# Sign convolutions in blocks of 16 rows across the images, in a fixed order, with shorter steps between the layers

## The chip, the cores and the metric

The kernel runs on one core of a Trainium2 chip, as one launch. The metric is the device time of that core in microseconds (us). The engines are named as in the profile: PE is TensorE's matmul, PEld its weight load, DVE the vector engine, ACT the scalar engine, POOL GpSimd, SP the engine that issues most transfers.

## The reference

The input is `x` of 16 images, 256 channels, 28 x 28 pixels in float32. Four layers follow one another. Cut to what matters here:

```python
# layer 0: sign of x, 3x3 convolution with the signs of the weights, batch norm, residual
y  = sat_conv2d(binary_activation(x), sign(w0)) * mean(abs(w0))   # the scale is per output channel
x  = (y - mean(y)) * rsqrt(var(y) + eps) * gamma + beta + x       # statistics over images and pixels
# layer 1: a 3x3 and a 1x1 convolution with real weights on signs, gates, PReLUs
...
# layer 2: two sign convolutions with batch norms before, between and after
out = sign(batchnorm(x, g1, b1))
out = prelu(binconv(out, w1), a1)          # weights sign(w1) * mean(abs(w1))
out = sign(batchnorm(out, g2, b2))
out = prelu(binconv(out, w2), a2)
x   = prelu(batchnorm(out, g3, b3) + x, a3)
# layer 3: attention over the 784 pixels of each image, then a projection, plus x
```

So there are three sign convolutions of the same size: one in layer 0, two in layer 2. Each is followed by statistics over all images, and nothing of the next part can begin before these are known.

## The kernel before

Channels lie on 128 partitions, in two halves `k` of the input and `mo` of the output. `S` = 28, `N` = 784, `HN` = 392, `HR` = 14, `B` = 16.

A sign convolution adds whole numbers. Of the 18 pairs of input half and tap, 15 are computed with *packed* weights: the signs for one output half plus 4095 times those for the other, so that one matmul serves both. ACT and DVE get the upper number out by rounding, and an *unpack* matmul takes it away again from one half and adds it to the other. The last three pairs are computed plainly, once for each output half.

```python
def sign_conv(pss, pad, w, temp):
    def product(ps, h, lhsT, n, t, start, stop, again=False):
        k, g = CHUNKS[n]
        r, c = divmod(3 * g + t, 3)
        T.matmul(ps[:, h, :HN]..., lhsT=lhsT,                      # line 198
                 rhs=pad[:, k, r + h * HR:r + h * HR + HR, c:c + S], start=start, stop=stop, ...)
    bs = [None, None]
    for h in range(2):                                             # two halves of an image
        for n in range(5):
            for t in range(3):
                product(pss[0], h, w[0][:, n, t, :], n, t, n + t == 0, n + t == 6)
        r, bs[h] = temp("t1"), temp("up", FR)
        A.activation(r, pss[0][:, h, :HN], AF.Identity, bias=rounding, scale=1.0 / PACK)   # line 210
        V.tensor_scalar(bs[h], r, -ROUND, None, ALU.add)           # line 211
    for h in range(2):
        for mo in range(2):
            for t in range(3):
                product(pss[mo], h, w[1][:, t, mo * P:(mo + 1) * P], 5, t, ...)
    for h in range(2):
        for mo in range(2):
            T.matmul(pss[mo][:, h, :HN], lhsT=unpack[mo], rhs=bs[h], start=False, stop=True, ...)  # line 218
```

An image takes 30 packed, 12 plain and 4 unpack matmuls. Each image has a padded buffer of its own (two, in turn), and the order of instructions on each engine is chosen by the framework's scheduler. The weights' signs and their mean absolute values come in six chunks:

```python
def sign(k, g):
    st = sts[k, g] = load_taps(pool, src, k, g, *stage)
    ...                                                            # the sixth chunk: plain signs
    A.activation(sg, st, AF.Sign, saturate=False)                  # line 158
    V.scalar_tensor_tensor(dst[0][:, n], sg[:, :, P:], PACK, sg[:, :, 0:P], ALU.mult, ALU.add)
def add_up(k, g):
    V.tensor_reduce(ab, st.rearrange("p t o -> p o t"), AX.X, ALU.add, apply_absolute_value=True)  # line 169
    part = acc.tile([P, 2], F32, tag="sm", name="sumabs")
    for mo in range(2):
        T.matmul(part[:, mo:mo + 1], lhsT=ab[:, mo * P:(mo + 1) * P], rhs=ones, start=True, stop=True)  # line 172
    ...                                                            # DVE adds part to the total
```

In layer 2 a convolution's result goes through a PReLU, and its statistics are taken:

```python
def conv2(i, b, w, beta):
    pss_ = [conv_ps() for mo in range(2)]
    sign_conv(pss_, pads2[i % 2], w, temp)
    for mo, ps in enumerate(pss_):
        r = ph.tile([P, 2, HN], F32, tag="r", name="r", bufs=3)
        ...
            A.activation(r[:, h], ps[:, h, :HN], AF.Relu, scale=-1.0)                # line 710
            V.scalar_tensor_tensor(p[:, h], r[:, h], beta[:, mo:mo + 1], ps[:, h, :HN], ALU.mult, ALU.add)
            for j in range(h.start, h.stop):
                V.bn_stats(stats[:, mo, 2 * b + j, :], p[:, j, :])                   # line 715
steps = [rest[1]] + both(*sign_weights(ph, w2b, d["w2b"], sf2, pss, ("r", 3)))     # the stage is the buffers of r
sign2a(0)
for i in range(B):
    if i + 1 < B:
        sign2a(i + 1)                                              # also loads image i + 2 from memory
    conv2(i, order[i], w2a, r1)
    if i >= 2 and steps:
        steps.pop(0)()
m, v = mean_var("l2b", stats)
keep_busy(m, 9)
sg2, bg2 = sign_bn("l2b", sf1, m, v, pv("g2"), pv("b2"))
```

`mean_var` aggregates all 32 partial statistics of each half and copies mean and variance; `sign_bn` is a chain of small DVE operations around one square root on ACT. `keep_busy` issues useless matmuls whose operand is made from the mean:

```python
def keep_busy(v, n):
    A.copy(idle[:, 0:2], v)                                        # line 285
    ps = pss.tile([P, 512], F32, tag="sm", name="unused")
    for _ in range(n):
        T.matmul(ps, lhsT=idle[:, 0:P], rhs=idle, start=True, stop=True)   # line 288
```

In the attention each image's denominators are inverted, the values are normalized, and two ACT passes add up the denominators and their inverses so that an overflow is noticed (line 929, tile `junk`).

Of the kernel before, what the change touches and what calls it, by code (L numbers as in the profile page):

```python
# [36 lines left out]
P = 128  # L37
B = 16
# [8 lines left out]

PACK = 4095.0
# [16 lines left out]
def conv_seq_kernel(ctx: ExitStack, tc: tile.TileContext, d: dict, out: bass.AP):  # L65
# [19 lines left out]

    pads = [const.tile([P, 2, S + 2, S + 2], BF16, tag=f"pad{i}", name=f"pad{i}") for i in range(2)]
    for p in pads:
        nc.gpsimd.memset(p, 0.0)

    def float_pads(pool, tag):  # L90
        ps = [pool.tile([P, 2, S + 2, S + 2], FR, tag=f"{tag}{i}", name=f"fpad{i}") for i in range(2)]
        for p in ps:
            nc.gpsimd.memset(p.bitcast(F32), 0.0)
        return ps
# [4 lines left out]
    eye = wpool.tile([P, P], F32, tag="wa", name="eye")  # L99
    make_identity(nc, eye)  # L100
    unpack = [wpool.tile([P, P], FR, name=f"unpack{i}") for i in range(2)]
    for u, f in zip(unpack, (-PACK, 1.0)):
        V.tensor_scalar(u, eye, f, None, ALU.mult)
    rounding = const.tile([P, 1], F32, name="rounding")
    nc.gpsimd.memset(rounding, ROUND)
# [8 lines left out]
    def inv_std(name, var):  # L114

        v, r, t = vtile(name + "_v"), vtile(name + "_r"), vtile(name + "_t")
        V.tensor_scalar(v, var, EPS, None, ALU.add)
        A.activation(t, v, AF.Sqrt)
        V.reciprocal(r, t)
        tt(t, r, r, ALU.mult)  # L120
        tt(t, t, v, ALU.mult)
        V.tensor_scalar(t, t, -0.5, 1.5, ALU.mult, ALU.add)
        return tt(r, r, t, ALU.mult)

    def affine(name, inv, gamma, beta, mean):

        s, c = vtile(name + "_s"), vtile(name + "_c")
        tt(s, gamma, inv, ALU.mult)
        tt(c, mean, s, ALU.mult)
        tt(c, beta, c, ALU.subtract)  # L130
        return s, c
# [13 lines left out]
    def sign_weights(pool, dst, src, total, acc, stage=("st", 2), spare_dve=False):  # L145


        chunks = CHUNKS
        sts = {}

        def sign(k, g):
            st = sts[k, g] = load_taps(pool, src, k, g, *stage)
            n = chunks.index((k, g))
            if n == 5:
                A.activation(dst[1], st, AF.Sign, saturate=False)
                return
            sg = pool.tile([P, 3, 256], BF16, tag="t1", name="sg", bufs=2)
            A.activation(sg, st, AF.Sign, saturate=False)
            V.scalar_tensor_tensor(dst[0][:, n], sg[:, :, P:], PACK, sg[:, :, 0:P], ALU.mult, ALU.add)  # L159

        def add_up(k, g):
            st = sts.pop((k, g))
            ab = pool.tile([P, 256], F32, tag="ab", name="ab", bufs=2)
            if spare_dve:
                A.activation(st, st, AF.Abs)
                nc.gpsimd.tensor_tensor(ab, st[:, 0, :], st[:, 1, :], ALU.add)
                nc.gpsimd.tensor_tensor(ab, ab, st[:, 2, :], ALU.add)
            else:
                V.tensor_reduce(ab, st.rearrange("p t o -> p o t"), AX.X, ALU.add, apply_absolute_value=True)
# [23 lines left out]
    def sign_conv(pss, pad, w, temp):  # L193

        def product(ps, h, lhsT, n, t, start, stop, again=False):
            k, g = CHUNKS[n]
            r, c = divmod(3 * g + t, 3)
            T.matmul(  # L198
                ps[:, h, :HN].rearrange("p (a b) -> p a b", b=S), lhsT=lhsT,
                rhs=pad[:, k, r + h * HR:r + h * HR + HR, c:c + S], start=start, stop=stop,  # L200
                skip_group_check=again,
            )

        bs = [None, None]
        for h in range(2):
            for n in range(5):
                for t in range(3):
                    product(pss[0], h, w[0][:, n, t, :], n, t, n + t == 0, n + t == 6)
            r, bs[h] = temp("t1"), temp("up", FR)
            A.activation(r, pss[0][:, h, :HN], AF.Identity, bias=rounding, scale=1.0 / PACK)  # L210
            V.tensor_scalar(bs[h], r, -ROUND, None, ALU.add)  # L211
        for h in range(2):
            for mo in range(2):
                for t in range(3):
                    product(pss[mo], h, w[1][:, t, mo * P:(mo + 1) * P], 5, t, mo == 1 and t == 0, False, mo == 0)
        for h in range(2):
            for mo in range(2):
                T.matmul(  # L218
                    pss[mo][:, h, :HN], lhsT=unpack[mo], rhs=bs[h], start=False, stop=True,
                    skip_group_check=(mo == 0),  # L220
                )

# [3 lines left out]
    def row_parts(first):  # L226

        return ((0, HR + 1), (HR + 1, S)) if first else ((0, S),)

    def img(ap):  # L230
        return ap.rearrange("p (a b) -> p a b", b=S)

    def mean_var(name, st):

        m, v = vtile(name + "_m"), vtile(name + "_var")
        for k in range(2):
            mv = small.tile([P, 2], F32, tag="mv", name="mv")
            V.bn_aggr(mv, st[:, k].rearrange("p c s -> p (c s)"))
            V.tensor_copy(m[:, k:k + 1], mv[:, 0:1])
            V.tensor_copy(v[:, k:k + 1], mv[:, 1:2])  # L240
        return m, v

    def sign_bn(name, sf, m, v, gamma, beta):

        t = vtile(name + "_sv")
        tt(t, sf, sf, ALU.mult)
        tt(t, t, v, ALU.mult)
        r = inv_std(name, t)
        tt(r, r, sf, ALU.mult)
        return affine(name, r, gamma, beta, m)  # L250
# [7 lines left out]
    stats = const.tile([P, 2, 2 * B, 6], F32, name="stats")  # L258
# [15 lines left out]
    with tc.tile_pool(name="ps_conv", bufs=3, space=PSUM) as psc, \  # L274
# [6 lines left out]
        nc.gpsimd.memset(idle[:, 2:], 0.0)  # L281

        def keep_busy(v, n):

            A.copy(idle[:, 0:2], v)
            ps = pss.tile([P, 512], F32, tag="sm", name="unused")
            for _ in range(n):
                T.matmul(ps, lhsT=idle[:, 0:P], rhs=idle, start=True, stop=True)

        with tc.tile_pool(name="ph1", bufs=1) as ph:  # L290

            pads0 = float_pads(ph, "vs")
# [10 lines left out]
            def sign0(b):  # L303
                for r in row_parts(b == 0):
                    for k in range(2):
                        A.activation(
                            inner(pads0[b % 2], k, *r), img(xs[b][:, k, :])[:, r[0]:r[1]], AF.Sign, saturate=False
                        )

            def quarter(tag, dt=F32):  # L310
                return ph.tile([P, HN], dt, tag=tag, name=tag, bufs=2)
# [3 lines left out]
            sign0(0)  # L315
            for s in signs:
                s()
            load_x(1)

# [24 lines left out]
            steps = [lambda k=k, c=c: w1_step(k, c) for k in range(2) for c in range(3)] + [fw_step] + sums_  # L344
            for b in range(B):
                if b + 1 < B:
                    sign0(b + 1)
                if b + 2 < B:
                    load_x(b + 2)
                n = ph.tile([P, 2, N], I16, tag="n", name=f"n{b}", bufs=2)  # L350
                pss_ = [conv_ps() for mo in range(2)]
                sign_conv(pss_, pads0[b % 2], w0, quarter)
                for mo, ps in enumerate(pss_):
                    for h in range(2):
                        V.bn_stats(stats[:, mo, 2 * b + h, :], ps[:, h, :HN])
                    A.copy(halves(n[:, mo, :]), ps[:, :, :HN])
                nc.gpsimd.dma_start(out=n0d[b], in_=n)
                if b >= 2 and steps:
                    steps.pop(0)()
# [3 lines left out]


            s1, c1 = affine("abn1", inv_std("abn1", pv("a_bn1_3")), pv("a_bn1_0"), pv("a_bn1_1"), pv("a_bn1_2"))
            s2, c2 = affine("abn2", inv_std("abn2", pv("a_bn2_3")), pv("a_bn2_0"), pv("a_bn2_1"), pv("a_bn2_2"))
            s3, c3 = affine("fbn1", inv_std("fbn1", pv("f_bn1_3")), pv("f_bn1_0"), pv("f_bn1_1"), pv("f_bn1_2"))
            s4, c4 = affine("fbn2", inv_std("fbn2", pv("f_bn2_3")), pv("f_bn2_0"), pv("f_bn2_1"), pv("f_bn2_2"))
            cc = tt(vtile("cc"), c2, c4, ALU.add)

            m0, v0 = mean_var("l0", stats)
            keep_busy(m0, 16)
            sc0, bi0 = sign_bn("l0", sf0, m0, v0, pv("g0"), pv("b0"))
            zb1 = tt(vtile("zb1"), bi0, pv("a_move"), ALU.add)

            ra1, ra2, rf2 = (combine("r" + q, pv(q), -1.0, 1.0) for q in ("a_alpha1", "a_alpha2", "f_alpha2"))
            ns1, ns3, nc3, nbi0 = (combine(q, v, -1.0) for q, v in (("ns1", s1), ("ns3", s3), ("nc3", c3), ("nbi0", bi0)))
            zb2 = tt(vtile("zb2"), c2, pv("f_move"), ALU.add)
# [5 lines left out]
            mix_x, mix_y, mix_c, s24 = (const.tile([P, 2, 2], F32, name=n) for n in ("mix_x", "mix_y", "mix_c", "s24"))  # L384
            w_1, w_2, b_1 = (ph.tile(sh, F32, name=n) for sh, n in (([P, 2, P], "se1"), ([P, 256], "se2"), ([64, 1], "seb")))
            hidden = [ph.tile([P, 2], F32, name=f"hidden{i}") for i in range(3)]
            for t in (w_1, w_2, *hidden):
# [819 lines left out]
```

## Time and profile before

The time is 1230.58 us, the median of three runs from 1229.44 to 1232.80. The profiled execution spans 1228.1 us with 15404 instructions.

| Engine | busy us | share | instructions |
|---|---|---|---|
| PE | 1125.3 | 92% | 5940 |
| PEld | 934.6 | 76% | 5944 |
| DVE | 784.3 | 64% | 1405 |
| ACT | 691.5 | 56% | 1047 |
| POOL | 140.9 | 11% | 131 |

The stages, from the timeline (the first useful matmul of a stage to its last): layer 0 from 20.25 to 169.0 us, layer 1 from 179.72 to about 563.5, the two convolutions of layer 2 from 580.96 to 747.3 and from 757.81 to 904.5, the attention from 917.99 to the end. A matmul's record lasts longer than the distance from one start to the next[...]; a short wait of PE doesn't show as idle time, and the distance of the starts has to be read.

### The profile page before, as it was taken

Reading aid. Unit: us, or ns where it says so; the run is one execution under the profiler, and the core shown is the slowest. Engines: PE = TensorE matmul, PEld = TensorE weight load, DVE = VectorE, ACT = ScalarE, POOL = GpSimd, SP = SyncE. Lnnn points to the kernel's source line nnn. Section 1 sums busy time; section 2 is a strip of 40 time slices with the busy share of each in tenths; the row PEclk is TensorE's granted clock in tenths of the full one; section 3 lists DMA queues with packets and bytes.
Section 4 is the critical chain, followed back from the end, with each engine's and each line's share of the span. In section 5 each row is a group of like instructions: output and inputs, shape, how many; then the busy total and the mean of one; then the engine's idle time right before and its main releaser. Section 6 shows DMA issues by size and latency. Waiting matters only on the chain.

```text
span 1228.1 us, 15404 instructions
## 1 busy us (share of the span) xinstructions
PE 1125.3 (92%) x5940; PEld 934.6 (76%) x5944; DVE 784.3 (64%) x1405; ACT 691.5 (56%) x1047; POOL 140.9 (11%) x131
## 2 busy tenths in 40 slices
PE   5999989999999999984987997999979999999995
PEld 4999969999899999983976996999955455455542
DVE  5563359999999998965444544454563665565565
ACT  3564435757676665654534543545547767667642
POOL 2000000000100000001000000000003333324412
PEclk9999999999999999995998998999989999999997
DMA  6454321222221321101322320000003544553512
GB/s 261 147 195 153 123 101 43 77 104 89 109 79 66 119 80 53 46 33 66 131 78 85 125 79 1 1 1 1 1 1 105 132 135 102 158 147 106 143 79 81
DMA packets 25967, 111.61 MB, mean 91 GB/s; under 512 B 3552, under 2 KB 6304, under 8 KB 25888
## 3 DMA queue, kind: packets, MB, share of 16 engines
q1 hardware_dynamic: 20432, 80.85, 18.5%
q0 software_dynamic: 5456, 29.71, 8.6%
q8 instruction: 49, 0.80, 0.3%
q14 instruction: 30, 0.25, 0.1%
HBM read 65.59 MB, written 44.96 MB: 90 GB/s over the span
## 4 chain that ended last, share of the span: by engine, by line
PE 74%; DVE 12%; ACT 10%; issue 2%; DMA 1%; POOL 1%; SPq 0%; ACTq 0%; POOLq 0%; DVEq 0%
PE cv L198 32%; PE cv L468 15%; PE av L898 6%; PE sc L877 5%; PE mi L862 4%; PE sm L935 3%; PE cv L218 2%; DVE x L597 1%; ACT y L543 1%; DVE x L552 1%; ACT junk L929 1%; DVE stats L599 1%; ACT rn L428 1%; PE cv L565 1%; DVE xs L460 1%
## 5 line engine op out<-in xcount | busy, mean ns | idle before, releaser
L468 PE MATMUL cv<-vs,w 128*128 128x392 f32 x1536 | 301.7, 355 | 8.3 <-DVE y L501 7.2
L198 PE MATMUL cv<-fpad,wpk 128*128 128x392 f32 x1440 | 302.3, 358 | 0.8 <-DVE wpk L159 0.8
L468 PEld LDWEIGHTS cv<-vs,w 128*128 128x128 f32 x1536 | 286.2, 190 | 12.7 <-DVE y L501 9.9
L198 PEld LDWEIGHTS cv<-fpad,wpk 128*128 128x128 f32 x1440 | 271.8, 192 | 11.5 <-ACT t L210 7.7
L210 ACT ACTIVATE t<-cv,rounding 128x392 f32<-128x392 f32 x96 | 56.3, 587 | 168.5 <-PE cv L198 165.0
L198 PE MATMUL cv<-fpad,wpl 128*128 128x392 f32 x576 | 138.5, 368 | 13.7 <-DVE p L711 9.7
L198 PEld LDWEIGHTS cv<-fpad,wpl 128*128 128x128 f32 x576 | 105.2, 194 | 32.2 <-ACT t L210 17.4
L211 DVE TENSOR_SCALAR up<-t 128x392 fp32r<-128x392 f32 x96 | 34.8, 362 | 132.6 <-ACT t L210 130.9
L711 DVE SCALAR_TENSOR_TENSOR p<-r,r,cv 128x784 f32<-128x784 f32 (+1 forms) x66 | 63.6, 1002 | 86.2 <-ACT r L710 86.2
L881 ACT ACTIVATE es<-sc 112x784 f32<-112x784 f32 x112 | 86.9, 819 | 47.6 <-PE sc L877 47.5
L877 PE MATMUL sc<-q,k 64*112 64x392 f32 x448 | 90.1, 515 | 6.0 <-ACT es L881 4.4
L898 PE MATMUL av<-es,va 112*64 112x392 f32 x448 | 80.8, 499 | 0.0
L877 PEld LDWEIGHTS sc<-q,k 64*112 64x112 f32 x448 | 36.4, 174 | 47.8 <-ACT es L881 15.7
L869 DVE COPY k<-mi 64x784 f32<-64x784 f32 x16 | 15.6, 976 | 85.0 <-ACT q L868 85.0
L898 PEld LDWEIGHTS av<-es,va 112*64 112x64 f32 x448 | 29.3, 136 | 47.8 <-issue 45.0
L111 DVE TENSOR_TENSOR vs<-pad 128x840 fp32r<-128x840 bf16 (+1 forms) x68 | 64.1, 974 | 0.0
L715 DVE BATCH_NORM_STATS2 stats<-p 128x6 f32<-128x392 f32 x128 | 63.1, 553 | 0.0
L891 POOL TENSOR_TENSOR sum<-sum,es 112x784 f32<-112x784 f32 x32 | 59.7, 1866 | 2.5
L582 ACT ACTIVATE u<-cv,fbn_c,fbn_s 128x784 f32<-128x784 f32 x31 | 31.2, 1005 | 46.3 <-PE cv L565 46.3
L565 PE MATMUL cv<-z,fw 128*128 128x392 f32 x256 | 51.5, 351 | 5.1 <-ACT z L556 5.0
L710 ACT ACTIVATE r<-cv 128x784 f32<-128x784 f32 (+1 forms) x66 | 49.1, 790 | 10.2 <-PE cv L218 7.7
L565 PEld LDWEIGHTS cv<-z,fw 128*128 128x128 f32 x256 | 47.0, 194 | 6.0 <-ACT z L556 5.5
(232 smaller groups left out, 1593.4 us busy)
## 6 DMA issues: line engine op xcount, KB each, us to landing
xs<-in_x_dram SPq DMA_DIRECT2D x32, 784.0 KB, 4.4
x2d<-x POOLq DMA_DIRECT2D x16, 784.0 KB, 3.6
x<-x2d SPq DMA_DIRECT2D x16, 784.0 KB, 4.3
xd<-p SPq DMA_DIRECT2D x16, 784.0 KB, 3.3
out_dram<-p SPq DMA_DIRECT2D x15, 784.0 KB, 4.3
p<-x2d POOLq DMA_DIRECT2D x13, 784.0 KB, 8.6
n0d<-n POOLq DMA_DIRECT2D x16, 392.0 KB, 2.9
n<-n0d SPq DMA_DIRECT2D x16, 392.0 KB, 3.0
```

The source lines that it names most:

```text
L111: V.tensor_tensor(o, a, b, op)
L198: T.matmul(ps[:, h, :HN].rearrange("p (a b) -> p a b", b=S), lhsT=lhsT, rhs=pad[:, k, r + h * HR:r + h * HR + HR, c:c + S], start=start, s ...
L210: A.activation(r, pss[0][:, h, :HN], AF.Identity, bias=rounding, scale=1.0 / PACK)
L468: T.matmul(ps.rearrange("p (a b) -> p a b", b=S), lhsT=w[:, k, c, u, mo * P:(mo + 1) * P], rhs=vs[b % 2][:, u, k, :, c:c + S], start=(n == 0),
L565: T.matmul(ps[:, h, :HN], lhsT=w[:, k, mo * P:(mo + 1) * P], rhs=z2[b][:, k, h * HN:(h + 1) * HN], start=(n == 0), stop=(n == 3),)
L711: V.scalar_tensor_tensor(p[:, h], r[:, h], beta[:, mo:mo + 1], ps[:, h, :HN], ALU.mult, ALU.add)
L715: V.bn_stats(stats[:, mo, 2 * b + j, :], p[:, j, :])
L862: T.matmul(ps[:, h, :HN], lhsT=wqk[:, k, :], rhs=x[b][:, k, h * HN:(h + 1) * HN], start=(k == 0), stop=(k == 1),)
L877: T.matmul(ps[:MC, h, :HN], lhsT=k_[rows, c * MC:(c + 1) * MC], rhs=qs[b][rows], start=True, stop=True)
L881: A.activation(e, ps[:MC, :, :HN], AF.Exp, scale=0.125)
L891: (V if late else nc.gpsimd).tensor_tensor(sums[b, late], sums[b, late], e, ALU.add)
L898: T.matmul(ps[64 * h:64 * h + 64, :HN], lhsT=w, rhs=e[:, h, :], start=start, stop=stop)
```

## The change

The change is in four parts.

- **Blocks.** The padded images are stacked in a ring of three, with one row of zeros between two images. 16 images of 29 rows are 464 rows, or 29 blocks of 16, and a matmul takes one block of 448 columns. A block may lie in two images. Its plain and unpack products come after the next block's packed ones, so that the rounding in between has time.
- **Fixed order.** PE, ACT and DVE issue what a sign convolution emits in the order of the code.
- **Between the layers.** Statistics of the earlier blocks are aggregated ahead (`gather`), the norm has fewer small operations, constants are computed during layer 0, and the useless matmuls need no operand from the statistics.
- **Loads and attention.** The next weights are staged in the buffers of the images, images are loaded at once to where the results will lie, and the attention's passes over the denominators are moved to later places.

The core of the diff, with cuts:

```diff
-    def sign_conv(pss, pad, w, temp):
+    def sign_layer(ring, w, temp, sign, post, steps, moments):
...
+        def packed(j):
+            pss[j] = conv_ps()
             for n in range(5):
                 for t in range(3):
-                    product(pss[0], h, w[0][:, n, t, :], n, t, n + t == 0, n + t == 6)
+                    product(j, 0, w[0][:, n, t, :], n, t, n + t == 0, n + t == 6)
...
+            A.activation(r, pss[j][:, 0, :BN], AF.Identity, bias=rounding, scale=1.0 / PACK)
+            V.tensor_scalar(bs[j], r, -ROUND, None, ALU.add)
+
+        def plain(j):
             for mo in range(2):
                 for t in range(3):
...
+        with tc.manual_schedule(engines={ET.PE, ET.Activation, ET.DVE}):
+            for j in range(NBLK + 1):
+                if j == 0:
+                    sign_image(0)
+                if j < NBLK:
+                    packed(j)
+                if j > 0:
+                    plain(j - 1)
+                    post(j - 1, pss[j - 1], parts(j - 1))
+                if j == NBLK - 2:
+                    moments.gather()
+
+                while done + 1 < B and (j == 0 if done + 1 < RING else ...):
+                    done += 1
+                    sign_image(done)
+                if j >= 2 and steps:
+                    steps.pop(0)()
...
-        def keep_busy(v, n):
-            A.copy(idle[:, 0:2], v)
+        def keep_busy(n):
             ps = pss.tile([P, 512], F32, tag="sm", name="unused")
             for _ in range(n):
-                T.matmul(ps, lhsT=idle[:, 0:P], rhs=idle, start=True, stop=True)
+                tc.keep_in_program_order(T.matmul(ps, lhsT=idle[:, 0:P], rhs=idle, start=True, stop=True))
...
             load_x(0)
-            sign0(0)
-            for s in signs:
-                s()
+            for i in range(3):
+                signs[i]()
             load_x(1)
+            for i in range(3, 6):
+                signs[i]()
+            load_x(2)
...
-            steps = [...] + [fw_step] + sums_
+            steps = [...] + [fw_step] + sums_ + [constants]
...
+            for b in order[3:]:
+                x2[b] = pt[b]
+                nc.sync.dma_start(out=x2[b], in_=x2d[b])
...
+                def post(j, ps, parts):
+                    r = ph.tile([P, 2, BN], F32, tag="r", name="r", bufs=2)
+                    for mo in (slice(0, 1), slice(1, 2)) if j == NBLK - 1 else (slice(0, 2),):
+                        A.activation(r[:, mo], ps[:, mo, :BN], AF.Relu, scale=-1.0)
+                    for at, i, r0, r1, p0 in parts:
+                        n = (r1 - r0) * S
+                        for mo in range(2):
+                            p = pt[order[i]][:, mo, r0 * S:r1 * S]
+                            V.scalar_tensor_tensor(p, r[:, mo, p0:p0 + n], beta[:, mo:mo + 1], ps[:, mo, p0:p0 + n], ...)
+                            V.bn_stats(mom.part(at, mo), p)
...
-            steps = [rest[1]] + both(*sign_weights(ph, w2b, d["w2b"], sf2, pss, ("r", 3)))
+            steps = [rest[1]] + both(*sign_weights(xpool, w2b, d["w2b"], sf2, pss, ("x2", 3), tmp=ph, ab_tag="ab"))
...
-            keep_busy(m, 9)
-            sg2, bg2 = sign_bn("l2b", sf1, m, v, pv("g2"), pv("b2"))
+            keep_busy(30)
+            sg2, bg2 = norm("l2b", mom, pv("g2"), pv("b2"), sf1)
```

The numbers of useless matmuls go from 16, 9, 9 and 16 to 30, 20, 30 and 45. In the attention `watch` (the two ACT passes) is called after the next image's sums, and the last images' denominators come later than before.

## The prediction

> **What bounds the kernel now.** I read the page's chain of work first: TensorE is 74% of it, and line 198, the sign convolutions, is the largest entry. These convolutions are three of the five stages (layer 0 up to 169 us, and two in layer 2), so I asked for the busy time of each engine by stage (columns: window, length, PE, PEld, DVE, ACT, POOL with instruction counts, granted clock, DMA share, GB/s).
>
> ```profile
> PE 74%; DVE 12%; ACT 10%; issue 2%; DMA 1%; POOL 1%; SPq 0%; ACTq 0%; POOLq 0%; DVEq 0%
> ...
> 580.90:747.20 166.30, 152.70 (x765) 142.06 (x764) 77.82 (x142) 76.00 (x103) 0.00 (x0) 0.97 0.27 92
> 757.80:904.50 146.70, 146.58 (x738) 135.97 (x736) 67.99 (x122) 71.22 (x96) 0.00 (x0) 0.99 0.00 1
> 25.00:169.00 144.00, 142.70 (x725) 133.81 (x725) 62.91 (x147) 73.03 (x115) 8.79 (x15) 1.00 0.43 153
> ```
>
> Two of the three stages leave TensorE without idle time; the first convolution of layer 2 takes 166.3 us for the same arithmetic, 19.6 more than the second. So I asked two things of the timeline: what one matmul costs where TensorE never rests, and what happens where it does.
>
> ```profile
> 840.88 2.81 PE L198 MATMUL cv<-fpad,wpk 128*128 128x392 f32 x14
> 843.53 0.92 PE L198 MATMUL cv<-fpad,wpl 128*128 128x392 f32 x4
> 844.37 3.11 PE L198 MATMUL cv<-fpad,wpk 128*128 128x392 f32 x15
> 847.88 0.35 PE L198 MATMUL cv<-fpad,wpk 128*128 128x392 f32 x1
> 848.16 1.40 PE L198 MATMUL cv<-fpad,wpl 128*128 128x392 f32 x6
> 849.40 0.71 PE L218 MATMUL cv<-up,unpack 128*128 128x392 f32 x3
> ```
>
> The first column is the start. 14 starts from 840.88 to 843.53 are 189 ns apart; unpack matmuls, whose moving operand is flat, are 180 apart (849.40 to 849.94 for three). The jump from 847.88 to 848.16 is 0.28: a wait for ACT's rounding, hidden because a record (358 ns) outlasts the distance of two starts. There are two such jumps in an image, and each is followed by another long one; together 0.37 us. An image is 42 x 0.189 + 4 x 0.181 + 0.37 = 9.03 us, against 9.06 in the chain (831.98 to 841.04).
>
> ```profile
> 746.55 0.70 PE L218 MATMUL cv<-up,unpack 128*128 128x392 f32 x3
> 747.11 1.21 ACT L710 ACTIVATE r<-cv 128x784 f32<-128x784 f32 x2 [1.85 <-PE cv L218]
> 747.96 1.56 DVE L711 SCALAR_TENSOR_TENSOR p<-r,r,cv 128x784 f32<-128x784 f32 x2 [2.31 <-ACT r L710]
> 749.44 1.50 DVE L715 BATCH_NORM_STATS2 stats<-p 128x6 f32<-128x392 f32 x3
> ...
> 754.75 3.62 PE L288 MATMUL unused<-idle 128*128 128x512 bf16 x8 [7.50 <-ACT idle L285]
> 756.57 4.40 ACT L689 ACTIVATE fpad<-p,l2b_c,l2b_s 128x420 fp32r<-128x420 f32 x6 [1.80 <-DVE l2b_c L111]
> ```
>
> This is the end of a stage: ReLU, PReLU, statistics, then a chain of 0.16 to 0.20 us operations, and 10.9 us without a useful matmul. The useless ones come after 7.5 us of idleness.
>
> ```profile
> 661.48 2.33 PE L198 MATMUL cv<-fpad,wpl 128*128 128x392 f32 x6 [2.37 <-DVE p L711]
> 664.77 1.04 DVE L169 TENSOR_REDUCE ab<-st 128x256 f32<-128x768 f32 x1 [0.52 <-DMA st<-in_w2b_dram]
> 664.83 0.85 ACT L158 ACTIVATE sg<-st 128x768 bf16<-128x768 f32 x1 [3.75 <-DMA st<-in_w2b_dram]
> 666.65 0.60 PEld L172 LDWEIGHTS sumabs<-ones,ab 128*128 128x128 f32 x4
> 666.83 0.50 PE L172 MATMUL sumabs<-ones,ab 128*128 128x1 f32 x4
> ```
>
> This is the loss of the slow stage: weights of the next convolution are loaded into buffers shared with the ReLU's output, ACT and DVE stand behind the DMA, and TensorE behind both.
>
> [...] useless matmuls of 512 columns start 427 ns apart after 4.3 and 7.5 us of idleness, and the six at 661.48 are slow after only 2.37. [...]
>
> **The change, part by part** (minus is gained, in us).
>
> *Blocks.* A layer goes from 736 matmuls of 392 columns to 29 x 23 = 667 of 448. Of 189 ns, [...] 9 are the rows (189 less 180, for 14 rows); [...] A block is 21 x 0.214 + 2 x 0.204 = 4.90, a layer 142 to 143.5, say 142.7, against 16 x 9.06 = 145.0. The waits for rounding vanish because a block's plain products come one block later. **-2.3 a layer, -7.** In return the second block needs the second image, whose signs ACT takes in fixed order after the first rounding: 0.2 + 0.64 + about 1.4 us. **+2.3 in each layer 2 convolution**, and 0.5 at each stage's end, where the gather (two aggregations of 240 values, some 1.2 each by the 192 values that take 1.0) stands before the last rounding. **+6.**
>
> *Start.* The first image's products before end at 34.1, as if the layer had begun at 34.1 - 9.1 = 25. DVE there does constants and sums before it packs weights (first packing at 19.54, though ACT's first weights land at 6.7). Now those come later. Weights land one per 1.0 us, with an image (2 us) put between: the fifth at about 12.7, then ACT 0.84, packing 0.55; first block done near 15, second at 20. That is a beginning at 20 - 2 x 3.2 = 13.6. **-11.**
>
> *Sums of weights in fixed order.* This is the step that I hold decisive. In an iteration the code emits packed products, plain products of the block before, its post-processing, signs of images, and then a step. A step that sums weights has a reduction on DVE and two small products on TensorE. In fixed order these stand ahead of the next block's products and wait for the reduction, which stands behind the post-processing of products that have only just ended. In layer 2, from the last unpack's start: 0.20 to ACT, ReLU of 896 values 0.91 (0.81 for 784, 0.50 for 392), PReLU and statistics 2 x (0.62 + 0.55) = 2.3 to 2.5, packing 0.55, reduction 1.03, handover 0.1, products 0.47: 5.7, less one distance of 0.2: 5.5 lost. Two of the seven steps pack nothing and lose 4.9: 37.6 in all. In layer 0 there is only statistics ahead (1.1 to 1.3): 0.2 + 1.2 + 1.03 + 0.1 + 0.47 - 0.2 = 2.8, six times, 17. **+38 and +17.** After 5 us without products the clock halves; it stayed so for 3 to 5.5 us after each end of a stage, half of which is lost. Not every time: **+10.** Layer 0's seven steps for other weights take DVE about 3.5 us beside 1.7 of its own per block of 4.9: **+1.5.**
>
> *Weights into other buffers.* The 19.6 us of the slow stage go, as its stage buffers are free early. Thirteen images (10.4 MB) are queued ahead of them, at some 350 GB/s (the fastest slices of this stretch reach 292 to 367) 30 us from about 574, just in time for the first step. **-19.5, and +1.**
>
> *Norm chains.* Late parts alone are aggregated at the end (0.4 for 1.9), four copies go, and two operations. From the last unpack to the next useful product: layer 0 11.0 to 8; into layer 2 3 less; the two others 10.9 to about 8.6, as the last block's DVE work queues behind the block before. 30 useless products of 0.213 (half of the slow 427 ns) are 6.4, 45 are 9.6, so they end ahead of the chain or with it. **-10.6.**
>
> *Attention.* ACT's two watching passes (0.60 + 0.62 in the chain per image) leave the place where the next exponentials wait; TensorE waits there only 0.25 us, twelve times. The last images' reordering saves the 2 us before the sums at 1200.16. **-5.**
>
> Sum: -7 + 6 - 11 + 66.5 - 18.5 - 10.6 - 5 = +20, or about 1251.
>
> **Rivals.** *(a) The fixed order costs nothing at the sums*: if the reduction finds room early, 55 us of waits and 10 of clock fall away, and the time is near 1185. For it speaks that everything else in the change removes waits; against it that the order on DVE is fixed too. *(b) The stage's end and beginning bound*: the queue of 13 images delays weights by ten or more us, ACT holds TensorE in every step, and the time passes 1265. For it speaks that this stage stood behind such loads before (3.75 us each); against it the early free buffers. *(c) Longer matmuls cost more than fewer ones save*: 3.6% more columns without the waits gone would be +5 a layer, about 1272. Against it speak the jumps in the steady timeline.
>
> **Range and chances.** I take 1246 rather than 1251, for rival (a) pulls harder than (b) and (c). Layer 0's start and sums may be off by 6 each, the clock by 10, which gives the upper end, 1268; the lower, 1203, holds much of (a). Below 1206 lies some 0.2, above 1255 some 0.3, between them 0.5.
>
> **What would show it.** Matmuls of 448 columns 213 to 216 ns apart; thirteen waits of TensorE for DVE's reduction, six near 2.4 us and seven near 5, with a lower clock after the latter; the first convolution of layer 2 at 185 to 200 us, the second at 145; the first block near 10 us; gaps between stages 2 to 3 us shorter. If those waits are absent or under 1 us, the central step is wrong and the time is under 1206.

## The result, and the profile after

The kernel after takes **1282.03 us** (median of 4 runs, 1281.05 to 1283.14) against 1230.01 for the kernel before in the same rounds: a ratio of **1.042, interval 1.040 to 1.044**. The profiled execution spans 1280.3 us, 52.2 more than before. The prediction was 1246, with a range up to 1268: the right side of zero, and too small.

First the page of the kernel after: the forty slices, each 32 us long, for TensorE and its granted clock.

```profile
PE   6967999999999999985665999999999999999996
...
PEclk9978999999999999997877999999999999999998
```

Away from the two ends, slices 2 and 3 (64 to 128 us, in layer 0) and slices 18 to 21 (576 to 704 us, the step into layer 2 and most of its first convolution) are the only places that are dark in both rows. TensorE is less busy there, and what it does it does at a lower clock. The windows of the three sign convolutions (columns as before: window, length, PE, PEld, DVE, ACT, POOL, granted clock, DMA share, GB/s) say the same in numbers:

```profile
8.70:191.60 182.90, 160.65 (x691) 138.71 (x693) 78.78 (x214) 82.46 (x141) 8.63 (x15) 0.94 0.40 141
601.80:807.40 205.60, 166.77 (x696) 145.14 (x698) 98.30 (x222) 84.56 (x107) 0.00 (x0) 0.88 0.19 73
814.70:960.70 146.00, 144.06 (x667) 126.21 (x669) 87.00 (x196) 80.01 (x101) 0.00 (x0) 1.00 0.00 1
```

The second convolution of layer 2, which sums no weights, has next to no idle time (144.06 of 146 us busy). The first does the same arithmetic and takes 205.6; it was 166.3 before. The new blocks cost what they should; this is TensorE's timeline where nothing disturbs it (`wpk` are the packed weights, `wpl` the plain ones, `unpack` those of the unpack products):

```profile
849.93 3.40 PE L243 MATMUL cv<-ring,wpk 128*128 128x448 f32 x15
853.17 1.46 PE L243 MATMUL cv<-ring,wpl 128*128 128x448 f32 x6
854.47 0.57 PE L262 MATMUL cv<-up,unpack 128*128 128x448 f32 x2
854.88 3.39 PE L243 MATMUL cv<-ring,wpk 128*128 128x448 f32 x15
```

15 packed products go from 849.93 to 853.17, or 216 ns apart; a block is 854.88 - 849.93 = 4.95 (4.93 over two blocks), and 29 x 4.93 = 143.0 us against 16 x 9.06 = 145.0 before. Now the same engine and its neighbours in the slow stage, in order of time (brackets give the idle time of the engine ahead of a line, and what ended it):

```profile
629.83 0.57 PE L262 MATMUL cv<-up,unpack 128*128 128x448 f32 x2
630.49 0.92 ACT L806 ACTIVATE r<-cv 128x896 f32<-128x896 f32 x1 [1.12 <-PE cv L262]
...
631.44 0.68 DVE L811 SCALAR_TENSOR_TENSOR p<-r,r,cv 128x448 f32<-128x448 f32 x1 [1.64 <-ACT r L806]
632.15 0.63 DVE L814 BATCH_NORM_STATS2 l2b_parts<-p 128x6 f32<-128x448 f32 x1
632.70 0.66 DVE L811 SCALAR_TENSOR_TENSOR p<-r,r,cv 128x448 f32<-128x448 f32 x1
633.39 0.63 DVE L814 BATCH_NORM_STATS2 l2b_parts<-p 128x6 f32<-128x448 f32 x1
633.94 0.54 DVE L197 SCALAR_TENSOR_TENSOR wpk<-sg 128x384 fp32r<-128x384 bf16 x1
634.40 1.02 DVE L208 TENSOR_REDUCE ab<-st 128x256 f32<-128x768 f32 x1
...
635.48 1.01 PE L211 MATMUL sumabs<-ones,ab 128*128 128x1 f32 x4 [5.07 <-DVE ab L208]
...
636.35 5.58 PE L243 MATMUL cv<-ring,wpk 128*128 128x448 f32 x15
...
641.76 1.46 PE L243 MATMUL cv<-ring,wpl 128*128 128x448 f32 x6
```

Read it downward: the unpack products end a block; ACT's ReLU follows, then two pairs of PReLU and statistics on DVE, the packing of weights, and only then the reduction. TensorE waits 5.07 us for it, for the sake of four records of one column each. The next 15 packed products need nothing that is late: their signs have long been there. But they stand behind the sums in TensorE's order. And when they start, they run from 636.35 to 641.76, 5.41 us instead of 3.24: the granted clock is 0.50 from 634.46 to 641.29. The list of waits (waiting tile, releaser, us in all, times, longest) adds it up:

```profile
PE sumabs L211 <- DVE ab L208: 55.7, 13, 5.7
```

Thirteen such waits, as the sums have thirteen steps. In the kernel before, the same wait reads:

```profile
PE sumabs L172 <- DVE ab L169: 3.8, 5, 1.3
```

Two of these five lie ahead of the first product, where TensorE has nothing else to do, and the three in layer 2 are 0.4 to 0.5 us each.

At the end of a stage the useless products now begin at once, where before they came after 7.5 us of idleness:

```profile
807.38 6.42 PE L354 MATMUL unused<-idle 128*128 128x512 bf16 x29
```

After them the first useful product starts at 814.77; 0.97 of that gap is a wait. The gap from 807.31 to 814.77 is 7.5 us long, against 10.6 before (747.25 to 757.81).

### The profile page after: what moved, and what is told of

The parts are those of the page before. It is cut to its first block, busy times and chain, and to the rows that moved or that the text cites. A ratio compares the mean times of both kernels' runs of the same rounds, so it can differ in the third digit from the quotient of the medians.

```text
span 1280.3 us, 15397 instructions
## 1 busy us (share of the span) xinstructions
PE 1158.5 (90%) x5808; PEld 931.2 (73%) x5812; DVE 818.1 (64%) x1539; ACT 711.3 (56%) x1067; POOL 137.4 (11%) x137
## 4 chain that ended last, share of the span: by engine, by line
PE 61%; DVE 13%; ACT 8%; issue 2%; POOL 1%; DMA 0%; ACTq 0%; DVEq 0%; POOLq 0%
PE cv L243 21%; PE cv L567 14%; PE av L992 6%; PE sc L971 6%; PE mi L956 3%; PE sm L1032 3%; PE mi L1042 2%; PE cv L262 2%; DVE p L811 1%; DVE x L696 1%; ACT y L642 1%; DVE x L651 1%; DVE l_parts L698 1%; ACT rn L527 1%; DVE xs L559 1%
## 5 line engine op out<-in xcount | busy, mean ns | idle before, releaser
L243 PE MATMUL cv<-ring,wpk 128*128 128x448 f32 x1305 | 324.7, 405 | 18.7 <-DVE unpack L394 8.8
L243 PEld LDWEIGHTS cv<-ring,wpk 128*128 128x128 f32 x1305 | 268.8, 208 | 57.1 <-issue 11.6
L254 ACT ACTIVATE t<-cv,rounding 128x448 f32<-128x448 f32 x87 | 54.9, 631 | 167.1 <-PE cv L243 167.1
L811 DVE SCALAR_TENSOR_TENSOR p<-r,r,cv 128x448 f32<-128x448 f32 (+15 forms) x172 | 87.1, 506 | 80.2 <-ACT r L806 80.2
L243 PE MATMUL cv<-ring,wpl 128*128 128x448 f32 x522 | 126.6, 379 | 0.0
L255 DVE TENSOR_SCALAR up<-t 128x448 fp32r<-128x448 f32 x87 | 34.0, 391 | 144.5 <-ACT t L254 144.4
L243 PEld LDWEIGHTS cv<-ring,wpl 128*128 128x128 f32 x522 | 99.4, 190 | 13.5
L806 ACT ACTIVATE r<-cv 128x896 f32<-128x896 f32 (+1 forms) x60 | 53.4, 893 | 57.7 <-PE cv L262 55.5
L473 ACT CAST n<-cv 128x896 int16<-128x896 f32 (+15 forms) x43 | 27.7, 645 | 60.7 <-DVE l_parts L472 57.8
L681 ACT ACTIVATE u<-cv,c_bn,s_bn 128x784 f32<-128x784 f32 x31 | 31.1, 1004 | 46.3 <-PE cv L664 46.3
```

The source lines that it names most:

```text
L243: T.matmul(pss[j][:, mo, :BN].rearrange("p (a b) -> p a b", b=S), lhsT=lhsT, rhs=ring[:, k, r:r + BR, c:c + S], start=start, stop=stop, sk ...
L254: A.activation(r, pss[j][:, 0, :BN], AF.Identity, bias=rounding, scale=1.0 / PACK)
L806: A.activation(r[:, mo], ps[:, mo, :BN], AF.Relu, scale=-1.0)
L811: V.scalar_tensor_tensor(p, r[:, mo, p0:p0 + n], beta[:, mo:mo + 1], ps[:, mo, p0:p0 + n], ALU.mult, ALU.add)
```

## The experiments

Theory: the weights' sums, put in fixed order behind a block's post-processing, hold TensorE thirteen times and halve its clock; all else in the change gains. Rivals: the stage is bound by the queue of 13 images or by ACT, so that TensorE would wait elsewhere if the sums did not hold it; or the fixed order itself, or some other part, costs the time. All diffs are against the kernel after, unless said otherwise. Each ratio is to the kernel before in the same rounds.

### 1. The sums' products two blocks later

```diff
-            part = acc.tile(...)          # in add_up: 2 matmuls, then DVE's addition to total
+            def product():                # the same, returned instead of called
+                part = acc.tile(...)
...
                 if j > 0:
                     plain(j - 1)
+                    if len(late) > 1 or (late and not steps):
+                        (late.pop(0) or (lambda: None))()
...
-                    steps.pop(0)()
+                    late.append(steps.pop(0)())
```

> The two small products that sum a chunk of weights are issued two blocks after DVE's reduction, behind that block's unpack products; everything else is as in the changed kernel. Theory (TensorE stands at these products, and its clock halves after): the thirteen waits of 2.1 to 5.7 us go, in all some 56 us, and with them the slow restarts (2.2 us in each of seven blocks of layer 2, 1.5 to 2.4 in four of layer 0, 22 in all): about 1205 us, and the first convolution of layer 2 takes some 150 us instead of 205. Rival (loads queued behind thirteen images, or ACT's signs, hold the layer): the waits move to other instructions and the time stays above 1240. Rival (the longer matmuls cost it): the time stays above 1230.

Measured: 1200.8 us, ratio 0.976 (0.975 to 0.978). The fixed order stays, the reductions stay where they were, and only the two small products and their addition move. The windows of layer 0 and of the first convolution of layer 2:

```profile
8.70:165.40 156.70, 151.50 (x691) 131.59 (x693) 78.05 (x214) 82.10 (x141) 8.63 (x15) 0.98 0.46 165
573.90:725.00 151.10, 147.37 (x695) 129.15 (x697) 96.68 (x221) 84.09 (x106) 0.00 (x0) 1.00 0.26 100
```

182.9 became 156.7 and 205.6 became 151.1, with the same counts of instructions to within one and the clock back at 0.98 and 1.00. The line of waits for the reduction is gone. **81 us of time hang on the place of 26 products of one column each (52 records).** The first rival would have shown waits of the same size elsewhere, and there are none: the largest new one is 1.8 us.

### 2. The waits kept, the clock kept up

```diff
+            if not spare_dve:
+                keep_busy(9 if total is sf0 else 23)
             part = acc.tile([P, 2], F32, tag="sm", name="sumabs")
```

> The sums stay where they are; in front of each pair of their products TensorE gets useless matmuls of 512 columns, 9 in layer 0 (some 1.9 us) and 23 in layer 2 (4.9 us), about as long as its wait there. Theory: the waits stay, the clock no longer halves, so only the slow restarts go: 1282 less 22 to 25, near 1258. If the halved clock has no part in it, the time stays at 1282 or rises a little; if waits alone are a smaller part than I think, it falls below 1245.

Measured: 1259.81 us, ratio 1.024 (1.022 to 1.025). It is 22.2 us faster than the kernel after, though it issues 215 more matmuls. TensorE's timeline:

```profile
657.31 0.57 PE L266 MATMUL cv<-up,unpack 128*128 128x448 f32 x2
657.73 5.14 PE L360 MATMUL unused<-idle 128*128 128x512 bf16 x22
663.50 0.58 PE L213 MATMUL sumabs<-ones,ab 128*128 128x1 f32 x4 [0.64 <-DVE ab L208]
663.94 3.50 PE L247 MATMUL cv<-ring,wpk 128*128 128x448 f32 x15
```

The reduction still comes late, most of the idle time is merely filled, and the sums and the 15 products behind them are nearly as fast as in an undisturbed block (0.58 instead of 1.01, 3.34 from start to start instead of 5.41; 3.24 undisturbed; the page's granted clock is 0.9 or more in every slice from 629 to 1226 us). So of some 81 us, 22 are the clock, and the rest the waits and the sums' own time.

### 3. No fixed order

```diff
-        with tc.manual_schedule(engines={ET.PE, ET.Activation, ET.DVE}):
+        with nullcontext():
```

> The changed kernel without the fixed order in the sign convolutions: the scheduler chooses the order on TensorE, ACT and DVE as it did before the change. Theory: blocks, ring, early gather and short norms remain, and the sums find gaps of their own: 1195 to 1225. If the fixed order was not what made the sums wait, the time stays within 10 us of 1282.

Measured: 1187.49 us, ratio **0.965 (0.964 to 0.967)**; layer 0 takes 149.4 us and the first convolution of layer 2 148.6. That is below the 1195 to 1225 that were expected. One line of the source is worth 94.5 us. Where the sums go when the compiler's scheduler places them:

```profile
621.78 0.81 PE L243 MATMUL cv<-ring,wpk 128*128 128x448 f32 x3
622.42 0.50 PE L211 MATMUL sumabs<-ones,ab 128*128 128x1 f32 x4
622.79 2.82 PE L243 MATMUL cv<-ring,wpk 128*128 128x448 f32 x12
```

They stand between the third and the fourth packed product, where their reduction is done: no wait, and they cost the 0.37 us that they take (622.42 to 622.79).

### 4. Fixed order again: sums late, second image early

This is experiment 1 with two more edits.

```diff
                 if j == 0:
                     sign_image(0)
+                    done = 1
+                    sign_image(1)
...
-                    ns[b] = ph.tile([P, 2, N], I16, tag="n", name=f"n{b}", bufs=2)
+                    tag, bufs = ("rn", 4) if b == 0 else ("n", 2)
+                    ns[b] = ph.tile([P, 2, N], I16, tag=tag, name=f"n{b}", bufs=bufs)
```

> The later sums, and beside them two small things: the second image's signs are emitted ahead of the first block's rounding, and the first image of layer 1 gets its integers in a buffer that is free early. Theory: 1.65 us less at the start of each convolution of layer 2, some 1.5 in layer 0, and some 2 to 4 at the start of layer 1 (a wait of 1.83 us for a transfer and a slow restart): 7 to 9 us less than the run with later sums alone. If TensorE finds other waits there, less than 3.

Measured: 1192.48 us, ratio 0.969 (0.967 to 0.970). The wait of 1.65 us for the second image (at 607.01 in the kernel after) is gone from both convolutions of layer 2. What remains in fixed order is a trace of the first rival:

```profile
596.75 0.84 ACT L196 ACTIVATE sg<-st 128x768 bf16<-128x768 f32 x1 [7.89 <-DMA st<-in_w2b_dram]
...
598.17 1.55 PE L247 MATMUL cv<-ring,wpl 128*128 128x448 f32 x6 [1.70 <-ACT t L258]
```

The signs of the next weights wait 7.89 us for their load, ACT keeps its order meanwhile, and the rounding behind it keeps TensorE waiting for 1.70. A second wait of 1.77 follows at 602.27. The loads behind 13 images were real, but hidden behind the larger waits.

### 5. Free order, useless products from the start, layer 1's integers early

Experiment 3, with useless products ahead of the first block and the first image's integers in another buffer.

```diff
+        nc.gpsimd.memset(idle, 0.0)
...
             load_x(0)
+            keep_busy(34)
...
-                    ns[b] = ph.tile([P, 2, N], I16, tag="n", name=f"n{b}", bufs=2)
+                    tag, bufs = ("rn", 4) if b == 0 else ("n", 2)
+                    ns[b] = ph.tile([P, 2, N], I16, tag=tag, name=f"n{b}", bufs=bufs)
```

> The run with free order (1187.5 us), and in it 34 useless matmuls at the very start of the program, so that TensorE's clock is up when the first products come, and the first image of layer 1 gets its integers in a buffer that is free early. Theory: in the run with free order the first two blocks take some 10.5 us of which half a block's time is lost to the slow clock, and layer 1 waits 1.8 us for a transfer and restarts slowly: 3 to 6 us less, 1182 to 1185. If the useless matmuls hold up the sums of weights in front of the first products, 0 to 3 us more.

Measured: 1187.35 us, ratio 0.964 (0.962 to 0.965): a miss, no gain over experiment 3. Layer 0 runs faster (147.8 for 149.4; its first nine packed products take 2.28 us, where the first three of experiment 3 took 1.47) but begins later, at 11.42 for 9.34, so its end moves from 158.76 to 159.22. In layer 1 the wait ahead of the first product falls from 1.77 to 0.66, and with the later end of layer 0 the product starts only 0.64 earlier, at 166.71.

### 6. Free order without the useless products

```diff
-            keep_busy(30)        # and (20), (30), (45): all four calls at the stages' ends
```

> The run with free order without any useless matmul between the layers. Theory: at each of four places TensorE is idle for 7 to 11 us and starts with half its clock, which costs 2 to 2.7 us each: 1187.5 plus 7 to 11, near 1196. Rival (the useless matmuls end too late and hold up the useful ones, or the clock falls all the same): within 3 us of 1187.5.

Measured: 1193.68 us, ratio 0.969 (0.968 to 0.971), so the useless products are worth 6.2 us. The end of the first convolution of layer 2, first with them (experiment 3), then without:

```profile
717.77 6.42 PE L354 MATMUL unused<-idle 128*128 128x512 bf16 x29
724.59 4.62 PE L243 MATMUL cv<-ring,wpk 128*128 128x448 f32 x20 [0.40 <-ACT ring L789]
```

```profile
719.86 0.57 PE L262 MATMUL cv<-up,unpack 128*128 128x448 f32 x2
727.31 2.24 PE L243 MATMUL cv<-ring,wpk 128*128 128x448 f32 x5 [6.88 <-ACT ring L787]
```

The gap is no longer without them: from the start of the last unpack products to the first packed one it is 7.45 us (719.86 to 727.31), and 7.46 with them (717.13 to 724.59). But the first five products behind it take 2.24 us, where with them the first twenty take 4.62, and the whole second convolution takes 145.8 us instead of 143.3.

### 7. The attention's watching passes back in their old place

```diff
         V.tensor_tensor(o[:, n], o[:, n], r[:, n], ALU.mult)
+        watch(b, n)
...
-            if b > 1:
-                watch(b - 2)
```

The later calls fall away; experiment 3 otherwise.

> The run with free order, with the attention's two watching passes put back right behind the normalization, as before the change. The trace of the changed kernel shows the same 0.27 us wait for the exponential in each image, and 18.13 us an image as before. Theory now: the wait is set by TensorE's own scores and the exponential behind them, so it costs nothing: within 1.5 us of 1187.5. The step of the prediction (3 us from these passes) would make it 1190.5.

Measured: 1188.46 us, ratio 0.965 (0.963 to 0.966), not separable from experiment 3. Moving the passes brought nothing.

### 8. and 9. The early aggregation of statistics

Experiment 8 calls the gathering at the end instead of two blocks ahead; experiment 9 keeps all parts in one tile and aggregates them once. Both in free order.

```diff
-                if j == NBLK - 2:
-                    moments.gather()
...
+            self.gather()                 # 8: first thing in get()
...
-                V.bn_aggr(self.mv[:, k, :], self.fin[:, k, :])
+                V.bn_aggr(self.mv[:, k, :], self.parts[:, k].rearrange("p c s -> p (c s)"))   # 9
```

> The run with free order, with the early statistics aggregated at the end of each stage, in front of the norm, and not two blocks ahead. Theory: two aggregations of 1.12 us and one product stand in each of four chains, 2.4 us each, less what the chain waits for anyway: 1187.5 plus 7 to 10. Rival (the aggregation ahead delays the last blocks as much): within 3 us.

> The run with free order, with all partial statistics of a stage aggregated at once at its end, as before the change: the run before this one only moved the call, and the scheduler put the instruction back to where it was. Theory: two aggregations of about 1.25 us stand in each of four chains where two of 0.22 stood: 2 us each, 1187.5 plus 6 to 8, near 1194. If the aggregation ahead is worth nothing: within 2 us.

Experiment 8 says nothing: 1187.11 us, ratio 0.963 (0.961 to 0.965), because the scheduler put the early aggregation back to where it was (714.16 us, against 714.37 in experiment 3). Its operands were still ready early. Experiment 9 takes that freedom away and gives 1193.06 us, ratio 0.968 (0.967 to 0.970): some 5.6 us are what the early aggregation brings. In its timeline on DVE, one aggregation of 258 values for each half of the channels stands on the path:

```profile
722.25 2.48 DVE L148 BATCH_NORM_AGGREGATE l2b_mv<-l2b_parts 128x2 f32<-128x258 f32 x2
```

In experiment 3 the two at this place are `128x21` and take 0.36.

### 10. and 11. Loads spread out, in free and in fixed order

Four images are loaded ahead and the others one at a time as images are signed; 10 is otherwise experiment 3 with the integers of experiment 5, and 11 is experiment 4.

```diff
-            for b in order[3:]:
-                x2[b] = pt[b]
-                nc.sync.dma_start(out=x2[b], in_=x2d[b])
+            for i in range(3, 7):
+                load_pt(i)            # the same three lines for one image
+            # in the callback that signs image i: load_pt(i + 5); for i = 2, image 7
```

> The run with free order, with four of layer 2's thirteen images loaded ahead and the other nine one by one as the convolution goes on, so that the next weights do not queue behind 10 MB; and layer 1's first integers in a buffer that is free early. Theory (rival b in small): ACT's wait of up to 7.9 us for the first weights goes, and with it 1 to 3 us of TensorE: 1184 to 1187. If the queue costs nothing here: 1187 to 1188.

> The fixed order with later sums and the second image early (1192.5 us), with the same spread loads. Theory (rival b in small): the two waits of 1.70 and 1.77 us that TensorE has behind ACT's first wait for weights go: 1189. If they move elsewhere: 1192.

Experiment 10: 1187.23 us, ratio 0.964 (0.962 to 0.965), no gain in the whole. Experiment 11: 1190.51 us, ratio 0.965 (0.964 to 0.967), 2.0 under experiment 4; the waits of 7.89, 1.70 and 1.77 us are gone and the stage is 148.3 for 150.7. So the queue of 13 images costs some 2 us in fixed order, and nothing that shows where the scheduler can put other work ahead. Fixed order, repaired three times, comes to within about 3 us of the free one; the intervals of 10 and 11 overlap. Its layer 0 stays 4.4 us longer than in free order (153.8 for 149.4 in experiment 3). Part of this can be seen: in free order three of layer 0's six sums stand at 8.50, 10.68 and 13.94, where TensorE waits for weights anyway (they take 0.44 us each in fixed order), and in fixed order TensorE waits 1.64 us for ACT's signs at 64.05. The rest, some 1.4 us, is not explained.

## Why the prediction went wrong

The stages before and after, and the best of each order (us; first product to the end of the last one):

| Kernel | layer 0 | layer 1 begins | layer 2, conv 1 | layer 2, conv 2 | span |
|---|---|---|---|---|---|
| before | 148.8 | 179.72 | 166.3 | 146.7 | 1228.1 |
| after | 182.8 | 200.14 | 205.4 | 145.9 | 1280.3 |
| fixed order repaired (11) | 153.8 | 169.91 | 148.3 | 143.7 | 1188.7 |
| free order (3) | 149.4 | 167.35 | 148.6 | 143.3 | 1185.5 |

The prediction's terms against what the two traces show:

| Term | predicted | measured | from |
|---|---|---|---|
| waits and products of the sums, layer 2 | +38 | +43.9 | seven losses of 6.1 to 6.6 |
| the same, layer 0 | +17 | +22.9 | six: 6.7, 2.8, 3.9, 2.9, 3.8, 2.9 |
| halved clock after them | +10 | +22.6 | 15 products in up to 5.7 for 3.24: 15.5 and 7.1 |
| start of layer 0 | -11 | -7.9 | second block's packed products done at 23.45, not 20 |
| other steps, blocks and tail of layer 0 | -0.3 | +0.4 | rest of that stage |
| layer 2, conv 1: weights, blocks, second image, tail | -18 | -20.3 | rest of that stage |
| layer 2, conv 2: blocks, second image, tail | +0.5 | -0.8 | stage table |
| norm chains (four gaps) | -10.6 | -11.1 | 2.1 + 2.4 + 3.1 + 3.5, from the last product's end |
| layer 1 | 0 | +2.9 | a slower start and end |
| attention | -5 | -0.5 | first product to the end |
| sum | +20.6 | +52.2 | span +52.2 |

A loss here is from where the next packed product would have started, 0.41 after the start of the two unpack products, to where it did start: 636.35 - 630.24 = 6.11 in the timeline above. It holds the wait and the sums' own time.

What failed is the price of the sums in fixed order: waits, products and clock together were put at +65 and came to +89.4. The gains at the start and in the attention fell short by 3.1 and 4.5; what the other terms were off by nearly cancels.

**The sums of weights.** The step failed in its size, not its mechanism. The prediction named it as the decisive one, saw thirteen waits in the right places and for the right reason, and experiment 1 confirms the cause. Its chain was short by three items. The handover from the last unpack's start (630.04) to ReLU is 0.45, not 0.20. The sums' four records take 0.87 to the next start, not 0.47, as they too run at a granted clock of 0.50. And a block that lies in two images splits into four pairs of PReLU and statistics, so that its loss is 6.6; that is also why the first and the last step, which pack nothing but fall on such blocks, still lose 6.14 and 6.16. (The working's own seven losses add up to 37.3, not 37.6, and the shorter idle time that it reads ahead of useless products was 4.5 us, not 4.3; neither matters here.) In layer 0 three of the six losses are the predicted 2.8. The two-image blocks give 3.8 and 3.9, for DVE's statistics and ACT's copy of the same tile alternate there, each waiting for the other. The brackets show it, in the timeline ahead of the loss of 3.80:

```profile
108.49 0.63 ACT L473 CAST n<-cv 128x560 int16<-128x560 f32 x1 [1.90 <-DVE l_parts L472]
109.15 0.52 DVE L472 BATCH_NORM_STATS2 l_parts<-cv 128x6 f32<-128x140 f32 x2 [0.75 <-ACT n L473]
...
109.58 1.02 DVE L208 TENSOR_REDUCE ab<-st 128x256 f32<-128x768 f32 x1
```

The first loss, 6.7, is another matter: ACT signs an image, and its first 17 rows once more for the other end of the ring, for 2.58 us (65.48 to 68.06). The cast of the step behind it and the next block's rounding come that much later, and with them DVE's work that stands ahead of the reduction.

**The clock.** The largest term that was mis-sized: 22.6 for 10. "Not every time" was wrong for layer 2, where all seven restarts are slow, at a granted clock of 0.50, each losing 1.9 to 2.4 us; and in layer 0 four of six are, losing 1.5 to 2.4, after 2.28 us of idleness already. Experiment 2 confirms it in another way: in the four steps of layer 2 from 645 to 690 us in its timeline the 15 products take 3.30 to 3.34 us, for 5.10 to 5.68 in the kernel after, and the sums 0.44 to the next start, for 0.84 to 0.87. In all it gains 22.2 us. In layer 0 its page still shows a granted clock of only 0.8 in the slice from 63 to 94 us.

**The start.** The first block was predicted near 10 us and its first product starts at 8.78, but the second block's 15 products take 5.77 us (17.68 to 23.45; 373 ns apart, as in layer 2 where the granted clock is 0.50), which the estimate of 20 left out. Experiment 5 shows that useless products ahead of the first ones gain nothing net here.

**Rival (a)**, the order costs nothing, put the time near 1185. The kernel was not that one, but with the order undone it is: 1187.5 in experiment 3. That is the rest of the prediction, right in sum to within a few us. **Rival (b)** was right about the queue of images and wrong about its size: 2 us (experiment 11), visible only once the sums are out of the way. **Rival (c)** is dead: 4.93 for a block, predicted 4.90 (from 214 ns a product, an estimate of mine whose split no trace shows; 216 were measured). The choice of 1246 over the sum of 1251 leaned toward (a) and cost another 5.

**The norm chains** came within a microsecond in all, which is partly luck: the single gaps are off by 0.6 to 1.2 us, two one way and two the other. Experiments 6 and 9 split the gain, though they were run in free order: 6.2 us for the useless products, 5.6 for the early aggregation. At the step into layer 1 a new wait took part of the place of the old one:

```profile
197.14 1.03 DVE L535 SCALAR_TENSOR_TENSOR xs<-n,l_r,xs 128x784 f32<-128x784 int16 x1 [1.83 <-DMA n<-n0d]
...
200.14 2.34 PE L567 MATMUL cv<-vs,w 128*128 128x392 f32 x8 [1.77 <-DVE vs L110]
```

The first image's integers are loaded into a buffer that is held until those of the last image but one have been stored, so the load goes out only at 193.56. That wait alone is not what slows layer 1: the same 1.77 us stand ahead of its first product in experiment 3 (167.35), and there 25 products take 4.98 us, some 193 ns apart. In the kernel after, the first five start 189 to 269 ns apart, and only from 200.97 on, where the granted clock falls to 0.50 until 204.38, are they 317 to 328 ns apart. This start costs 1.4 us of the +2.9. Most of the rest lies in the layer's last 32 records: behind a wait of 4.96 us, the same as before, the last 16 take 5.88 us for 4.90: the granted clock is 0.50 up to 586.67, where before it was 1.00 again after 3.5 us of them (at 562.10).

**The attention.** -5 was wrong. The wait that the watching passes were thought to cause is still there, of the same 0.27 us:

```profile
1069.24 1.54 ACT L975 ACTIVATE es<-sc 112x784 f32<-112x784 f32 x2 [1.03 <-PE sc L971]
1070.12 0.92 PE L971 MATMUL sc<-q,k 64*112 64x392 f32 x4 [0.27 <-ACT es L975]
```

ACT waited 1.03 us for TensorE's scores before these exponentials, so a pass ahead of them cannot be what makes them late. An image takes 18.13 us in both kernels. Experiment 7 agrees.

## What to carry to other kernels

Before fixing the order of an engine, ask of each instruction in the chain, however small, what its last operand waits for: here the sums' operand came behind a block's whole work on DVE, and issued at once they held everything behind them for up to 5.7 us; issued two blocks later they no longer waited for it. When such a wait is priced, the restart belongs to the price: here each wait of 5 us cost another 2.2 in clock. And read what else a scheduler was doing before it is switched off; here the change's other parts were worth 43 us, and its fixed order cost 94.5.

## What was not expected of the hardware

- The granted clock fell in shorter idle times than the 5 us that the prediction counted on. 2.28 us of idleness was followed by 15 products in 4.75 us once and in 3.33 once, and 2.13 by 3.29; all of the thirteen waits that were 3.2 us or longer were followed by 4.75 us or more.
- Two waits of the same 2.28 us ended differently. The changes of the granted clock in the trace of the kernel after lie multiples of 3.41 us apart (in layer 0 at 91.74, 95.16, 101.98, 105.39, 112.22 and 115.63). The wait that ended at 100.50 lay mostly in the step from 98.57 (95.16 + 3.41) to 101.98, and in the next step, to 105.39, the clock was 0.50; the one that ended at 120.09 was divided by the next edge, 119.05 (115.63 + 3.41), and the clock stayed at 1.00. Two cases don't show whether it is this that decides. In the first the clock fell after the work had begun again: from 101.23 to 101.88 the packed products start 215 to 220 ns apart, and from 102.17 to 105.16 they start 373 apart.
- At a granted clock of 0.50 these products did not cost double: they start 373 ns apart (636.87 to 640.97) instead of 216, or 5.6 us for 15. After each of the seven waits in layer 2 the clock is 0.50 for 6.82 or 6.83 us, part of it still in the wait, and the 15 products behind take 5.10 to 5.68 us for 3.24.
- Useless products in a wait that has to be waited anyway are worth more than they look: in experiment 2 they make no reduction come sooner and still bring 22.2 us.
